# A graph network in four layers on one core: the end of each attention row in nine steps instead of six

## The chip, the cores and the metric

The kernel runs on one core of one Trainium2 chip. The metric is the device time of one execution in microseconds (us), median of several runs. Five engines matter: TensorE (PE, with its weight loads shown apart as PEld), VectorE (DVE), ScalarE (ACT), GpSimd (POOL) and SyncE (SP), whose queue starts most of the transfers. Each engine takes its instructions in the order in which they were built; an instruction that waits holds up everything behind it on its engine.

## What is computed

Four graph layers work on x (4096 x 64) with one matrix adj (4096 x 4096). After each comes a residual sum and a layer norm. adj has some 1.6% entries that are not zero, all of them positive here. The part that matters is layer 1, in the reference:

```python
hw = h @ W
h_plus = (node_adj > 0).astype(hw.dtype) @ hw          # and h_minus for < 0
e_plus = leaky_relu(concat([h_plus, h_minus], 1) @ a)  # and e_minus
att = softmax(where(edge_adj > 0, e_plus, where(edge_adj < 0, e_minus, -9e15)), axis=1)
edge_support = att * edge_adj @ hw
edge_output = gru_cell(node_support, h, ...)           # from (A > 0) @ h and (A < 0) @ h
node_output = gru_cell(edge_support, h, ...)
x = layernorm(x + d_edge * edge_output + d_node * node_output)
```

Layer 0 is a Chebyshev filter (three products with adj), layer 2 a decaying sum over each row's last hundred neighbours, layer 3 a hyperbolic aggregation.

## The kernel before, in words

adj is handled in 8 groups of 512 rows by 8 chunks of 512 columns. Layer 0 turns every tile and puts it into device memory as adj_t; the later stages load tiles of 1 MB from there.

**Attention** (the function attention, L1022) goes through 64 tiles, groups 7 to 0, chunks 0 to 7 within each. I call the eight chunks of one group a row. For each tile:
- SP loads it (L1039 or load1, L482).
- DVE makes pos, a 0/1 copy of the positive entries (L489), two chunks ahead of its use, in a ring of three buffers.
- PE multiplies pos with the split features (wide, p_ps, L1080) and the tile itself with the features (weighed, a_ps, L1089), four and eight matmuls.
- ACT, or DVE on the diagonal, makes an fp8 mask of the nonzero entries (L1045, L1047), which goes out to mask_t for the decay stage.

When a row's eight chunks are summed, p_ps and a_ps are copied out (L1140, L1143), and what is left for these 512 nodes is small and sequential: the **row's end**, built by group_end (L825). Its parts run on alternating engines:
- edge_gates (PE, L853 and L860), edge_tanh (ACT, L869), edge_rest (DVE, L874 to L876);
- scores (DVE), tanh_n (ACT, L897) and score_exps (ACT, L924 and L925), shares (DVE), new_state for the edge (DVE, L900 to L902);
- gathered (PE, L950), shared, which writes gin (ACT, L959), node_gates (PE, L853), node_sum (DVE, L883), node_tanh (ACT, L887), node_rest (DVE, L892 and L894), tanh_n, new_state for the node;
- summed (DVE, L971 and L974) and the layer norm: statistics on DVE, a square root on ACT (L275, with a table load), the rest on DVE (L277 to L288);
- decay_parts, the split of the result into three bf16 parts (DVE, L243 to L247, L994), and decay_copies (POOL's queue, L1001).

The row's end isn't issued at once. It is a list of **steps**; one step is popped behind each chunk of the next row ("if steps: steps.pop(0)(ps_p)"), so that the small work lies among the matmuls. Before the change the list has six: the edge half, the gathering, the node half with the norm, nothing, decay_parts, decay_copies. The list of a row is appended behind its eighth chunk; steps that are left when the 64 tiles are done are issued then, one after the other. The first row carries four other steps. A scheduler then orders the instructions of each engine; most matmuls and the pos, mask and diagonal instructions keep the written order.

The positive and the signed case are two branches (If and Else) in the program; only the first runs here. At its end each engine jumps over the other branch to the **decay stage** (layer 2). There PE counts masks (cnt_ps, L1355), ACT (L1360) or DVE (L1362) turns a count into weights wt, and PE gathers with them. cnt_ps is one buffer for each half, so the next count waits until the wt before has read it. The end of the last group, group 0, is issued in that stage by the same group_end with by_ln=True, as 25 small steps (L1329).

Of the kernel before, what the change touches and what calls it, by code (L numbers as in the profile page):

```python
# [14 lines left out]
AF = mybir.ActivationFunctionType  # L15
# [47 lines left out]
def gnn4_kernel(  # L63
# [21 lines left out]
    nc = tc.nc  # L85
# [120 lines left out]
    def gblocks(g):  # L206
        return slice(g * GB, (g + 1) * GB)
# [48 lines left out]
    def over_rows(t, n=F):  # L256

        return t.unsqueeze(2).to_broadcast([P, GB, n])

    def layernorm(dst, y, by_ln=False, by_scale=False):  # L260

        st = sm.tile([P, GB, 6], F32, name="ln_st")
        mv = sm.tile([P, GB, 2], F32, name="ln_mv")
        for b in range(GB):
            nc.vector.bn_stats(st[:, b, :], y[:, b, :])
            nc.vector.bn_aggr(mv[:, b, :], st[:, b, :])
        ve = sm.tile([P, GB], F32, name="ln_ve")
        s = sm.tile([P, GB], F32, name="ln_s")
        r = sm.tile([P, GB], F32, name="ln_r")
        nc.vector.tensor_scalar_add(ve, mv[:, :, 1], LN_EPS)  # L270
        if by_ln:
            nc.scalar.activation(s, ve, AF.Ln)
            nc.scalar.activation(s, s, AF.Exp, scale=0.5)
        else:
            nc.scalar.activation(s, ve, AF.Sqrt)  # L275

        nc.vector.reciprocal(r, s)  # L277
        nc.vector.tensor_tensor(r, ve, r, ALU.mult)
        nc.vector.tensor_tensor(s, s, r, ALU.add)
        nc.vector.reciprocal(r, s)  # L280
        nc.vector.tensor_scalar_mul(r, r, 2.0)
        if by_scale:
            nc.vector.scalar_tensor_tensor(s, mv[:, :, 0], -1.0, r, ALU.mult, ALU.mult)
            for b in range(GB):
                nc.scalar.activation(dst[:, b, :], y[:, b, :], AF.Identity, bias=s[:, b : b + 1], scale=r[:, b : b + 1])
            return
        nc.vector.tensor_tensor(dst, y, over_rows(mv[:, :, 0]), ALU.subtract)
        nc.vector.tensor_tensor(dst, dst, over_rows(r), ALU.mult)  # L288

    def layernorm_steps(dst, y):  # L290

        mv = sm.tile([P, GB, 2], F32, name="ln_mv")
        ve = sm.tile([P, GB], F32, name="ln_ve")
        s = sm.tile([P, GB], F32, name="ln_s")

        def spread_of():
            st = sm.tile([P, GB, 6], F32, name="ln_st")
            for b in range(GB):
                nc.vector.bn_stats(st[:, b, :], y[:, b, :])
                nc.vector.bn_aggr(mv[:, b, :], st[:, b, :])  # L300
            nc.vector.tensor_scalar_add(ve, mv[:, :, 1], LN_EPS)

        def root():
            nc.scalar.activation(s, ve, AF.Ln)
            nc.scalar.activation(s, s, AF.Exp, scale=0.5)

        def normed():
            r = sm.tile([P, GB], F32, name="ln_r")
            nc.vector.reciprocal(r, s)
            nc.vector.tensor_tensor(r, ve, r, ALU.mult)  # L310
            nc.vector.tensor_tensor(s, s, r, ALU.add)
            nc.vector.reciprocal(r, s)
            nc.vector.tensor_scalar_mul(r, r, 2.0)
            nc.vector.tensor_tensor(dst, y, over_rows(mv[:, :, 0]), ALU.subtract)
            nc.vector.tensor_tensor(dst, dst, over_rows(r), ALU.mult)

        return spread_of, root, normed
# [40 lines left out]
    wih_pp = const.tile([P, H3 + 4], F32, name="wih_pp")  # L358
    wih_mm = const.tile([P, H3 + 4], F32, name="wih_mm")
# [157 lines left out]
    with tc.tile_pool(name="acc", bufs=1) as acc_p, tc.tile_pool(  # L517
# [10 lines left out]
        part = before.rearrange("p b f -> p (b f)")[:, 0 : N // 2].rearrange("p (b f) -> p b f", b=NB)  # L528
# [258 lines left out]
    nat_b = tr_a[:, N // 2 : N].rearrange("p (b f) -> p b f", b=NB)  # L787
    middle = ctx.enter_context(ExitStack())
    late = middle.enter_context(tc.tile_pool(name="late", bufs=1))
# [19 lines left out]
    last_p = [late.tile([P, GW], F32, name=f"last_p{q}") for q in range(2)]  # L809
    last_a = late.tile([P, GW], F32, name="last_a")  # L810
    wq = late.tile([P, 2, H3], F32, name="wq")
# [13 lines left out]
    def group_end(g, Q, nb, tl, sums, a_t, wq, by_ln=False):  # L825
# [8 lines left out]
        edge = tl.tile([P, GB, F], F32, name="edge")  # L834
        node = tl.tile([P, GB, F], F32, name="node")
        cnt = e[:, :, 2 : 2 + Q]
        xg = nat_a[:, gblocks(g), 0:F]
        got = {}
# [60 lines left out]
        def new_state(dst):  # L899
            nc.vector.tensor_tensor(dst, xg, n, ALU.subtract)  # L900
            nc.vector.scalar_tensor_tensor(dst, rz[:, :, F : 2 * F], 1.0, dst, ALU.add, ALU.mult)
            nc.vector.scalar_tensor_tensor(dst, dst, 0.5, n, ALU.mult, ALU.add)  # L902
# [75 lines left out]
        def normed(part):  # L978
            def step(ps_p):
                if part == 0:  # L980
                    got["norm"] = layernorm_steps(nat_b[:, gblocks(g), :], got["y"])
                got["norm"][part]()

            return step

        if by_ln:
            norm = [[summed, normed(0)], [normed(1)], [normed(2)]]
        else:
            norm = [[summed, lambda ps_p: layernorm(nat_b[:, gblocks(g), :], got["y"])]]

        def decay_parts(ps_p):

# [12 lines left out]
        def of(h, *parts):  # L1005
            return lambda ps_p: [part(ps_p, h) for part in parts]

        return [
            [of(0, edge_gates)], [of(0, edge_tanh)], [of(0, edge_rest), of(1, edge_gates)], [of(1, edge_tanh)],
            [of(1, edge_rest), scores], [tanh_n, score_exps], [shares], [lambda ps_p: new_state(edge)],  # L1010
        ], [
            [of(0, gathered)], [of(0, shared), of(1, gathered)], [of(1, shared)],
        ], [
            [of(0, node_gates)], [of(0, node_sum)], [of(0, node_tanh)], [of(0, node_rest), of(1, node_gates)], [of(1, node_sum)], [of(1, node_tanh)],
            [of(1, node_rest)], [tanh_n] + ([to_ln] if by_ln else []), [lambda ps_p: new_state(node)],
        ] + norm, [[nothing]], [[decay_parts]], [[decay_copies]]

    def steps_of(parts):

        return [lambda ps_p, part=part: [work(ps_p) for step in part for work in step] for part in parts]  # L1020

    def attention(signed, cols_p, sg, tl, ps_a, ps_p):  # L1022
# [86 lines left out]
        for n, (g, c) in enumerate(order):  # L1109
# [27 lines left out]
            if c == NCH - 1:  # L1137
                w_t = [tl.tile([P, GW], F32, name=f"p_t{q}") for q in range(Q)] if g else last_p
                a_t = tl.tile([P, GW], F32, name="a_t") if g else last_a
                nc.scalar.copy(w_t[0], wide_ps[0])  # L1140
                if signed:
                    nc.vector.tensor_copy(w_t[1], wide_ps[1])
                nc.scalar.copy(a_t, a_ps)  # L1143
                if g:
                    steps += steps_of(group_end(g, Q, 2, tl, list(zip(w_t, (wih_pp, wih_mm))), a_t, wq))
# [152 lines left out]
    with tc.tile_pool(name="mask2", bufs=3) as mk_p, tc.tile_pool(name="wt2", bufs=3) as wt_p, tc.tile_pool(  # L1298
# [18 lines left out]
        def gather_lo(jb, half, wt, acc):  # L1317
# [8 lines left out]
                ))  # L1326


        seam = steps_of(  # L1329
            [step]  # L1330
            for part in group_end(0, 2, 1, late, list(zip(last_p, (wih_pp, wih_mm))), last_a, wq, by_ln=True)
            for step in part
        )
        gathers = []
        busy = False
        for turn, groups in enumerate(turns_of):
# [71 lines left out]
    with tc.tile_pool(name="o3", bufs=1) as op, tc.tile_pool(name="cols3", bufs=3) as cols_p, tc.tile_pool(  # L1408
# [95 lines left out]
        def turn(n):  # L1504

            t, h = n
            i, j = tiles[t]
            work = []
            if i == j:
                tp = ps_p.tile([P, GW], F32, name="post", tag="post")  # L1510
                for k in range(HB):
                    for b in range(HB):
                        nc.tensor.transpose(tp[:, cols(HB * k + b)], fs[t][:, b, cols(HB + k)], ident)
                to = own[t][:, HB:CB, 0 : HB * P]
                work.append(lambda: nc.vector.tensor_tensor(to, tp.rearrange("p (k i) -> p k i", k=HB), to, ALU.mult))  # L1515
                return work
            for b in (HB * h, HB * h + 1):
                tp = ps_p.tile([P, GW], F32, name="post", tag="post")
                for k in range(CB):
                    nc.tensor.transpose(tp[:, cols(k)], fs[t][:, k, cols(b)], ident)  # L1520
                to = mirrored[t][:, b, :]
                work.append(lambda to=to, tp=tp: nc.vector.tensor_tensor(to, tp, to, ALU.mult))  # L1522
            return work
# [137 lines left out]
        while n < NU + 2 or turns or gathers:  # L1661
# [39 lines left out]
            late = turn(late_turns.pop(n)) if n in late_turns else []  # L1701
# [65 lines left out]
```

## Time and profile before

| | us |
|---|---|
| median of 3 runs | 1482.99 (1481.95 to 1486.22) |
| the profiled execution | 1476.74 |
| its span | 1474.4 |
| attention, from the first row's edge gates to the last adjacency matmul | 600.0 to 821.6 |
| decay stage | 822 to 1037 |
| hyperbolic layer | 1037 to 1474.4 |

The profile shows one execution. A line of the timeline or of the chain is: start, length, engine, source line, operation, what is written and read, how many; in brackets the idle time ahead of it and what ended it. A line of the waits is: who waited for whom, us in total, how often, the longest. The clock column is the share of full clock that TensorE was granted.

### The profile page before, as it was taken

The page shows a single profiled execution, that of the slowest core. Times are in us where ns is not written, and L with a number is a line of the kernel's source. Part 1 is how long each engine was busy: PE and PEld are TensorE (multiplying, and loading weights), DVE is VectorE, ACT ScalarE, POOL GpSimd, SP SyncE. Part 2 cuts the span into 40 slices and gives each one's busy share as a digit, 9 for nine tenths or more (in the row PEclk, how much of TensorE's full clock was granted, in tenths as well). Part 3 has the DMA queues.
Part 4 walks back from the last instruction along what each step waited for, and adds up shares of the span by engine and source line. Part 5 has one row for each costly group of instructions (what it writes and reads, how often), then busy time and mean ns, then how long its engine had stood idle before and what let it go on. Part 6 is the DMA issues. An engine that isn't in the chain of part 4 may idle for free.

```text
span 1474.4 us, 19118 instructions
## 1 busy us (share of the span) xinstructions
PE 1340.4 (91%) x6868; PEld 617.4 (42%) x6868; DVE 1050.0 (71%) x2008; ACT 804.0 (55%) x1331; POOL 108.4 (7%) x169
## 2 busy tenths in 40 slices
PE   5899999999999988899999899999788899988984
PEld 3455555555344323444444333333333334333443
DVE  5989998887343256666777312445999999999995
ACT  3554444433000114644432377554889999999993
POOL 4111111100133000011110000000000000000000
PEclk9999999999999999999999899999899999999997
DMA  9999999999589899979887645552525444534420
GB/s 288 410 410 410 410 409 397 388 366 353 212 334 370 317 387 373 358 271 348 314 300 269 207 129 179 163 173 66 214 114 195 176 175 164 211 143 182 165 93 11
DMA packets 105662, 385.35 MB, mean 261 GB/s; under 512 B 16341, under 2 KB 17369, under 8 KB 73561
## 3 DMA queue, kind: packets, MB, share of 16 engines
q1 hardware_dynamic: 85408, 298.87, 55.2%
q0 software_dynamic: 12736, 76.29, 12.7%
q10 hardware_dynamic: 7416, 8.90, 1.7%
q8 instruction: 56, 0.92, 0.3%
q14 instruction: 46, 0.37, 0.1%
HBM read 297.26 MB, written 85.20 MB: 259 GB/s over the span
## 4 chain that ended last, share of the span: by engine, by line
PE 53%; DVE 23%; ACT 15%; DMA 6%; issue 3%; ACTq 0%; DVEq 0%; SPq 0%
PE pass L553 7%; PE w_ps L553 6%; PE tp L645 6%; PE cnt_ps L1355 4%; PE a_ps L1089 4%; PE acc_ps L1311 4%; PE pass L546 3%; PE p_ps L1080 3%; DMA raw<-in_adj_dram 3%; DVE at_m L1522 3%; PE h_ps L546 2%; ACT w L1673 2%; PE post L564 2%; ACT wt L1360 2%; DVE rt L1698 2%
## 5 line engine op out<-in xcount | busy, mean ns | idle before, releaser
L652 ACT COPY at<-tp 128x512 f32<-128x512 f32 x256 | 132.3, 599 | 133.7 <-issue 92.0
L1360 ACT ACTIVATE wt<-cnt_ps 128x512 uint16<-128x512 f32 x208 | 115.5, 595 | 71.5 <-PE cnt_ps L1355 66.9
L645 PE MATMUL tp<-ident,raw 128*128 128x128 f32 x1024 | 131.3, 281 | 17.3 <-POOL state_hhn L386 6.7
L1536 PE MATMUL sums_ps<-at_d,some 128*64 128x512 f32 x288 | 144.0, 620 | 2.0 <-DVE at_d L1515 1.8
L678 DVE TENSOR_REDUCE dpart<-raw 128x4 f32<-128x2048 f32 x64 | 145.4, 2272 | 0.2 <-DMA raw<-in_adj_dram 0.2
L680 DVE TENSOR_REDUCE lows<-raw 128x1 f32<-128x2048 f32 x64 | 145.4, 2271 | 0.0
L645 PEld LDWEIGHTS tp<-ident,raw 128*128 128x128 f32 x1024 | 114.7, 143 | 56.9 <-issue 30.5
L1089 PE MATMUL a_ps<-at,nat_a 128*64 128x512 f32 x512 | 125.9, 619 | 3.7 <-DVE at L1058 3.7
L1548 PE MATMUL sums_ps<-at_m,some 128*64 128x512 f32 x224 | 110.2, 615 | 0.0
L553 PE MATMUL w_ps<-at,cheb_n 128*128 128x512 f32 x224 | 101.1, 595 | 0.0
L1475 PE MATMUL v_ps<-rv,tr_a 64*128 64x512 f32 (+1 forms) x288 | 79.8, 632 | 22.6 <-DVE rt L1698 22.4
L553 PE MATMUL pass<-at,cheb_n 128*128 128x512 f32 x224 | 98.3, 596 | 0.7 <-DVE cheb_n L706 0.7
L1698 DVE SCALAR_TENSOR_TENSOR rt<-v_ps,rt 128x1024 f32<-128x1024 f32 x72 | 83.1, 1154 | 4.8 <-ACT rt L1674 4.4
L1355 PE MATMUL cnt_ps<-m,follow 128*64 128x512 fp8e4 x480 | 81.7, 391 | 4.6 <-ACT wt L1360 2.1
L1683 DVE SCALAR_TENSOR_TENSOR f<-rt,w 128x1024 f32<-128x1024 f32 x72 | 82.8, 1155 | 3.1 <-ACT rt L1709 3.0
L1686 DVE TENSOR_TENSOR at_d<-at_d,f 128x1024 f32<-128x1024 f32 x72 | 82.9, 1151 | 0.1
L1362 DVE TENSOR_SCALAR wt<-cnt_ps 128x512 uint16<-128x512 f32 x48 | 33.2, 692 | 66.1 <-PE cnt_ps L1355 66.1
L1522 DVE TENSOR_TENSOR at_m<-post,at_m 128x512 f32<-128x512 f32 x112 | 74.5, 678 | 4.4 <-PE post L1520 4.3
L1709 ACT ACTIVATE rt<-rt 128x1024 f32<-128x1024 f32 x72 | 72.4, 1005 | 9.3 <-DVE rt L1698 9.0
L1520 PE MATMUL post<-ident,f 128*128 128x128 f32 x448 | 69.6, 285 | 7.4 <-DVE at_m L1522 6.4
L1673 ACT ACTIVATE w<-w 128x1024 f32<-128x1024 f32 x72 | 72.0, 1001 | 5.5 <-DVE w L1502 5.5
L546 PE MATMUL h_ps<-at,cheb_n 128*64 128x512 f32 x288 | 74.3, 602 | 0.0
(396 smaller groups left out, 2276.9 us busy)
## 6 DMA issues: line engine op xcount, KB each, us to landing
at<-adj_t SPq DMA_DIRECT2D x122, 1024.0 KB, 7.0
raw<-in_adj_dram SPq DMA_DIRECT2D x64, 1024.0 KB, 13.7
adj_t<-at POOLq DMA_DIRECT2D x64, 1024.0 KB, 8.0
at_d<-adj_t SPq DMA_DIRECT2D x36, 1024.0 KB, 4.6
at_m<-adj_t SPq DMA_DIRECT2D x28, 1024.0 KB, 6.7
m<-mask_t SPq DMA_DIRECT2D x120, 128.0 KB, 2.8
m<-mask_t SPq DMA_DIRECT2D x60, 256.0 KB, 3.8
mask_t<-mask ACTq DMA_DIRECT2D x28, 256.0 KB, 6.8
```

The lines of the kernel that those rows point to most:

```text
L546: in_order(nc.tensor.matmul(ps[q * F : (q + 1) * F, :], lhsT=cheb_n[:, jb, k, :], rhs=rhs, start=first, stop=last, skip_group_check=True,))
L553: in_order(nc.tensor.matmul(ps, lhsT=cheb_n[:, jb, k : k + 2, :], rhs=rhs, start=first, stop=last))
L645: in_order(nc.tensor.transpose(tp[:, cols(b)], raw[:, b, cols(k)], ident))
L652: nc.scalar.copy(at[:, k, :], tp)
L678: in_order(nc.vector.tensor_reduce(dpart[:, g, c, :], raw, AX.X, ALU.add))
L680: in_order(nc.vector.tensor_reduce(lows[:, n : n + 1], raw.rearrange("p b j -> p (b j)"), AX.X, ALU.min))
L1089: in_order(nc.tensor.matmul(ps[q * F : (q + 1) * F, :], lhsT=nat_a[:, c * CB + k, 0:F], rhs=of[q if signed else 0][:, k, :], start=(c == 0 ...
L1355: in_order(nc.tensor.matmul(cnt[a][r * HP : (r + 1) * HP, :], lhsT=follow, rhs=chunks[c][odd][2 * a + r][:, k, :], start=(h == 2 * NB - 1) ...
L1360: in_order(nc.scalar.activation(wt[odd][a], cnt[a], AF.Relu, scale=-128.0))
L1522: work.append(lambda to=to, tp=tp: nc.vector.tensor_tensor(to, tp, to, ALU.mult))
L1536: in_order(nc.tensor.matmul(bank[0:F, :], lhsT=nat_c[:, j * CB + k, :], rhs=own[t][:, k, :], start=(i == j and k == 0), stop=(j == seq[-1] ...
L1698: nc.vector.scalar_tensor_tensor(rt, vs[n][:, :, cs], (1.0 + V_FLOOR) * SCALE, rt, ALU.max, ALU.add)
```

## The change

- The row's end in attention is divided into nine steps instead of six. A step ends where another engine takes over; the two halves (h = 0, 1) of each part go together. One step is popped behind each chunk, as before.
- The layer norm of these rows is no longer one function but the three parts of layernorm_steps (statistics, root, rest); the root keeps Sqrt where by_ln is not set.
- The end of the last group (by_ln=True) has the same steps in the same order as before; only its list is written out in another way.

```diff
-    def layernorm_steps(dst, y):
+    def layernorm_steps(dst, y, by_ln):
...
         def root():
+            if not by_ln:
+                nc.scalar.activation(s, ve, AF.Sqrt)
+                return
             nc.scalar.activation(s, ve, AF.Ln)
             nc.scalar.activation(s, s, AF.Exp, scale=0.5)
...
-        if by_ln:
-            norm = [[summed, normed(0)], [normed(1)], [normed(2)]]
-        else:
-            norm = [[summed, lambda ps_p: layernorm(nat_b[:, gblocks(g), :], got["y"])]]
+        norm = [[summed, normed(0)], [normed(1)], [normed(2)]]
...
         return [
-            [of(0, edge_gates)], [of(0, edge_tanh)], [of(0, edge_rest), of(1, edge_gates)], [of(1, edge_tanh)],
-            [of(1, edge_rest), scores], [tanh_n, score_exps], [shares], [lambda ps_p: new_state(edge)],
-        ], [
-            [of(0, gathered)], [of(0, shared), of(1, gathered)], [of(1, shared)],
-        ], [
-            [of(0, node_gates)], [of(0, node_sum)], [of(0, node_tanh)], [of(0, node_rest), of(1, node_gates)], [of(1, node_sum)], [of(1, node_tanh)],
-            [of(1, node_rest)], [tanh_n] + ([to_ln] if by_ln else []), [lambda ps_p: new_state(node)],
-        ] + norm, [[nothing]], [[decay_parts]], [[decay_copies]]
+            [[of(0, edge_gates, edge_tanh), of(1, edge_gates, edge_tanh)]],
+            [[of(0, edge_rest), of(1, edge_rest), scores, tanh_n, score_exps]],
+            [[shares, lambda ps_p: new_state(edge), of(0, gathered), of(1, gathered)]],
+            [[of(0, shared, node_gates), of(1, shared, node_gates)]],
+            [[of(0, node_sum, node_tanh), of(1, node_sum, node_tanh)]],
+            [[of(0, node_rest), of(1, node_rest), tanh_n]],
+            [[lambda ps_p: new_state(node)], *norm[:2]],
+            [norm[2], [decay_parts]],
+            [[decay_copies]],
+        ]
```

More of the change, by code (lines that the diff above doesn't have):

```diff
@@ L980, in step @@
                 if part == 0:
-                    got["norm"] = layernorm_steps(nat_b[:, gblocks(g), :], got["y"])
+                    got["norm"] = layernorm_steps(nat_b[:, gblocks(g), :], got["y"], by_ln)
                 got["norm"][part]()
             return step
-        if by_ln:
-            norm = [[summed, normed(0)], [normed(1)], [normed(2)]]
-        else:
-            norm = [[summed, lambda ps_p: layernorm(nat_b[:, gblocks(g), :], got["y"])]]
+        norm = [[summed, normed(0)], [normed(1)], [normed(2)]]
         def decay_parts(ps_p):
@@ L1006, in of @@
             return lambda ps_p: [part(ps_p, h) for part in parts]
-        return [
-            [of(0, edge_gates)], [of(0, edge_tanh)], [of(0, edge_rest), of(1, edge_gates)], [of(1, edge_tanh)],
-            [of(1, edge_rest), scores], [tanh_n, score_exps], [shares], [lambda ps_p: new_state(edge)],
-        ], [
-            [of(0, gathered)], [of(0, shared), of(1, gathered)], [of(1, shared)],
-        ], [
-            [of(0, node_gates)], [of(0, node_sum)], [of(0, node_tanh)], [of(0, node_rest), of(1, node_gates)], [of(1, node_sum)], [of(1, node_tanh)],
-            [of(1, node_rest)], [tanh_n] + ([to_ln] if by_ln else []), [lambda ps_p: new_state(node)],
-        ] + norm, [[nothing]], [[decay_parts]], [[decay_copies]]
+        if by_ln:
+            return [[step] for step in [
+                [of(0, edge_gates)], [of(0, edge_tanh)], [of(0, edge_rest), of(1, edge_gates)], [of(1, edge_tanh)],
+                [of(1, edge_rest), scores], [tanh_n, score_exps], [shares], [lambda ps_p: new_state(edge)],
+                [of(0, gathered)], [of(0, shared), of(1, gathered)], [of(1, shared)],
+                [of(0, node_gates)], [of(0, node_sum)], [of(0, node_tanh)], [of(0, node_rest), of(1, node_gates)],
+                [of(1, node_sum)], [of(1, node_tanh)], [of(1, node_rest)], [tanh_n, to_ln],
+                [lambda ps_p: new_state(node)],
+            ] + norm + [[nothing], [decay_parts], [decay_copies]]]
+        return [
+            [[of(0, edge_gates, edge_tanh), of(1, edge_gates, edge_tanh)]],
[8 more added lines that the diff above has]
+        ]
     def steps_of(parts):
@@ L1326, in gather_lo @@
                 ))
[L1329 to L1333, printed above, removed]
+        seam = steps_of(group_end(0, 2, 1, late, list(zip(last_p, (wih_pp, wih_mm))), last_a, wq, by_ln=True))
         gathers = []
```

## The prediction

> **What bounds the kernel now.** I read the busy table first, then busy time in stretches, then the waits, the chain of waits, and last the timeline at the seam where attention hands over to the decay stage.
>
> ```profile
> PE 1340.4 (91%) x6868; PEld 617.4 (42%) x6868; DVE 1050.0 (71%) x2008; ACT 804.0 (55%) x1331; POOL 108.4 (7%) x169
> ```
>
> TensorE sets the pace, so a gain must come from its idle time or its clock. The changed path runs only in attention. Cutting that stage at each row's edge gates (L853) gives one stretch per row of eight chunks:
>
> ```profile
> 600.00:636.20 36.20, 31.79 (x134) 14.08 (x130) 23.77 (x71) 21.12 (x25) 5.64 (x4) 0.91 0.87 331
> 636.20:670.60 34.40, 30.75 (x132) 14.35 (x131) 23.41 (x71) 16.95 (x22) 3.38 (x4) 0.95 0.77 285
> 733.00:763.40 30.40, 28.86 (x130) 13.38 (x130) 23.68 (x71) 11.12 (x19) 3.73 (x4) 1.00 0.87 317
> 600.00:821.60 221.60, 203.86 (x888) 93.90 (x884) 161.76 (x494) 91.42 (x139) 25.99 (x28) 0.98 0.81 296
> ```
>
> Columns are length, then PE, PEld, DVE, ACT and POOL busy, the granted clock, DMA share, GB/s. PE idles 221.60 - 203.86 = **17.7 us**; the first two rows also ran below full clock. DVE is busy only 23.7 of 30.4 us in a row: it is not full, it is late. The waits name it, and the chain shows how:
>
> ```profile
> PE p_ps L1080 <- DVE pos L489: 12.0, 7, 3.1
> PE a_ps L1089 <- DVE at L1058: 3.7, 1, 3.7
> ```
> ```profile
> 743.82 0.39 DVE gin L883
> ...
> 746.03 0.43 ACT n L897
> ...
> 748.32 0.87 DVE y L974 x4
> ...
> 751.91 1.23 DVE first_pos L489
> 753.14 0.04 issue
> 753.18 2.33 PE p_ps L1080 x8
> 755.51 1.87 PE a_ps L1089 x8
> ```
>
> From 743.82 to 751.91, 8.1 us, DVE does one row's whole node half and norm, waiting twice for ACT; the next pos stands behind it. PE has two chunks of pos in hand, worth 2 x (1.12 + 1.87) = 6.0 us, and stands 1.5 us. By the gaps in PE's timeline the seven rows lose 4.4, 3.7, 3.2, 1.6, 1.5, 1.9 and 1.5 us, again 17.7.
>
> The seam today:
>
> ```profile
> 818.18 0.28 DVE L247 CAST sup_lo<-sp_rest 128x256 bf16<-128x256 f32 x1
> 819.62 1.94 PE L1089 MATMUL a_ps<-at,nat_a 128*64 128x512 f32 x8
> 821.60 0.59 ACT L1143 COPY last_a<-a_ps 128x512 f32<-128x512 f32 x1 [1.29 <-PE a_ps L1089]
> 822.96 0.69 DVE L1362 TENSOR_SCALAR wt<-cnt_ps 128x512 uint16<-128x512 f32 x1 [4.50 <-PE cnt_ps L1355]
> 824.57 0.60 ACT L1360 ACTIVATE wt<-cnt_ps 128x512 uint16<-128x512 f32 x1 [2.38 <-DMA m<-mask_t]
> 825.22 1.07 PE L1355 MATMUL cnt_ps<-at,follow 128*64 128x512 fp8e4 x4 [2.36 <-ACT wt L1360]
> ```
>
> DVE has finished its row work (sup_lo, 818.46) before the last adjacency matmul ends (821.56; call it T). The second count matmul waits until both wt have read the first: that is T + 3.7.
>
> **What the change removes: the clumps.** A row gets nine steps and a chunk pops one. On DVE the longest run without a pos becomes new state, sum and spread (746.48 to 750.27 in the row above, 3.8 us), or norm and split (1.7 + 1.9 = 3.6). Both are below 6.0. I walked the changed instruction order through the middle rows by hand with durations of that row. Each chunk is 1.12 + 1.87, edge gates 3.0, gathered 1.16, node gates 1.06. Each pos came out 2.9 us or more ahead of its matmul. So the idle goes, 17.7.
>
> The low clock goes with it: four p_ps took 2.07 in place of 1.12 and eight a_ps 3.22 in place of 1.87 right behind the 2.41 us gap at 625; eight a_ps took 3.81 behind the 3.65 us gap at 657. That is 0.95 + 1.35 + 1.94 = 4.2. Together **21.9 us** at most.
>
> I don't count all. In the row at 670 ACT's sqrt waited behind a mask pass whose load took 5.08 us in the chain, with DMA at 0.92; finer steps don't cure a late load, and denser PE work asks for loads sooner. I keep that row's 3.15 and one 0.55 wait for gin as not gained: 3.7. Gain 18.2 (bounds: 0, if ACT makes each pos as late as now, and 21.9).
>
> What is only regrouped costs nothing. Instructions are the same in number: 14 table loads before and after, 1.28 us each, all on ACT, which is busy 11 of 30 us. SP has the same loads, a few mask loads exchanged with a neighbour. POOL issues the same copies. Cover gone, one ACT table load late in a row would cost up to 1.3.
>
> **What it adds: a tail.** Nine steps against eight pops put each row one chunk further behind. Seven rows bring 63 steps; rows 6 to 0 pop 56. Seven steps of group 1 are left for the end, behind T. The built order confirms it: after the last a_ps PE has gathered and node gates, ACT gin, both tanh and the sqrt, DVE everything from node_sum to the bf16 split. All of it stands ahead of the engines' jump to the decay stage, and behind it in each queue wait the first wt. By rows of before:
> - edge gates end 3.0 us before T. From there to the last share, the row at 733 took 735.98 to 741.81, less two pos (2.3) that no longer stand among them, plus last_p's copy (0.59) ahead of the tanh: 4.1, so T + 1.1.
> - issue 0.1, then gin to the end of spread, 741.93 to 750.27: 8.3.
> - sqrt and norm to 751.99: 1.7. Split and bias, 754.18 to 757.29 less a pos (1.17): 1.9.
> - DVE is free at T + 13.1.
> - DVE's jump. No row shows it exposed. ACT's does: 2.38 us idle between last_a and its first wt, with the count matmul done at 822.86. Bounds 0 (DVE's sequencer could run ahead) and 2.4; I take 2.4, the same jump on the nearest engine.
> - wt 0.69: PE goes on at T + 16.2, in place of T + 4.2 (825.22 plus half of the cold 1.07).
>
> That is 12.0 later. But PE's gathered and node gates (1.16 + 1.06) no longer stand before T, so T itself is 2.2 earlier. **Tail 9.8** (7.4 if the jump is hidden). Behind it nothing else is late: mask loads for chunk 6 are issued from T + 0.9 and first used at 844.8, 19 us after the second count; POOL's copies of group 1 land in 2.5 us and serve blocks 4 to 7, near the end of the turn. PE is cold at the seam in both (0.52 granted from 825.2 to 835.0), so I add nothing for it.
>
> [...]
>
> **Sum.** -21.9 + 3.7 + 9.8 = **-8.4 us**. The profiled execution took 1476.74 (span 1474.4 plus 2.3 around it), which gives 1468.3. It lay 6.25 below the median 1482.99, to which the same difference gives **1474.6**. A measurement here tells a change from none from about 0.3% on, 4.4 us.
>
> **Rivals.**
> - *The tail eats the gain.* Each of the seven rows keeps 1.5 us, as the last rows show now, because a step's DVE part still waits for ACT with a pos behind it: 10.5 stay, gain 11.4, less 9.8: 1481.4. For it: seven ACT or PE waits a row remain on DVE, each ACT mask pass is 1.9. Against: the 2.9 us in hand.
> - *Slower.* The wait moves rather than goes: before each piece DVE waits for ACT, and ACT's queue has mask passes (1.9) and their DMA issues ahead of gin, tanh and sqrt. If two passes (3.8) stand there, the 2.9 in hand is used up in each row. It decides from the point where rows keep over 12.1 of the 21.9, since the tail's 9.8 is paid whatever they do. With 19 kept: +6.9, 1489.9. For it: the row at 670, where it happened. Against: in the changed order the passes that stand there are of chunks whose pos has already been made, so their data is in.
> - *All of it.* No stall left and DVE's jump hidden: -21.9 + 7.4 = -14.5, 1468.5. It is the forecast's lower end.
>
> **Chances.** Forecast with its lower end 0.62, tail eats it 0.25, slower 0.13. The forecast's own range is 1468 to 1478.5. For 8 in 10 the range takes in the first rival whole and the lower part of the slower one: 1468 to 1488; some 0.1 lies above it, 0.08 below. Faster by over 0.3% 0.62, within 0.25, slower 0.13.
>
> **What would show it.** Right: between the first edge gates and the last a_ps PE idles under 5 us, the wait of p_ps for pos nearly vanishes, the clock there is 1.00, and nine chunks with one row's steps take about 32 us. At the seam DVE's split ends some 13 us behind the last a_ps, and PE is idle for about 10 us ahead of the second count matmul. Wrong: gaps of 1.5 us in every row (first rival), DVE waits for ACT ahead of late pos (second), or a second count that doesn't wait for DVE, which would mean that the tail is covered and my 9.8 too large.

## The result and the profile after

Four runs took 1460.58 to 1465.81 us, median **1464.19**, beside a median of 1482.47 for the kernel before on the same chip: ratio 0.988 (95% interval 0.986 to 0.990), 18.3 us faster. The profiled execution took 1463.77 (span 1461.8), 13.0 less than that of before. The direction was as forecast (-8.4); the time is below the range.

Two places are to be compared: the rows of attention and the seam behind them. Line numbers of the changed kernel are higher by 3 from L306 on and by some 12 from attention on (pos L489 is L492, p_ps L1080 is L1092, the count L1355 is L1363).

Busy time in stretches of the kernel after, cut at the edge gates as before: length, then PE, PEld, DVE, ACT, POOL busy, the granted clock, DMA share, GB/s. A stretch is now nine chunks with one row's end; the last line is the whole stage up to the last adjacency matmul.

```profile
635.70:666.90 31.20, 31.20 (x141) 14.73 (x140) 27.43 (x78) 19.22 (x24) 3.84 (x5) 1.00 1.00 372
729.80:761.10 31.30, 31.30 (x144) 14.82 (x142) 25.85 (x73) 8.76 (x17) 4.19 (x5) 1.00 0.95 335
603.90:798.20 194.30, 194.30 (x871) 91.41 (x870) 152.79 (x453) 85.94 (x129) 19.98 (x24) 1.00 0.90 333
```

PE's busy time equals the length: no idle is left, and the granted clock is 1.00 in every row (nine chunks take 31.1 to 31.8 us). From the first edge gates to T the stage went from 221.2 to 194.3 us, 26.9 less. The waits of the same window show DVE ahead of PE where it had been late:

```profile
DVE pos L492 <- PE p_ps L1092: 7.6, 4, 3.5
```

The timeline of the kernel after at the seam (T is now 798.16):

```profile
796.22 1.94 PE L1101 MATMUL a_ps<-at,nat_a 128*64 128x512 f32 x8
...
804.42 1.16 PE L1363 MATMUL cnt_ps<-at,follow 128*64 128x512 fp8e4 x4 [2.85 <-issue]
...
811.15 0.29 DVE L247 CAST sup_lo<-sp_rest 128x256 bf16<-128x256 f32 x1
811.74 0.60 ACT L1368 ACTIVATE wt<-cnt_ps 128x512 uint16<-128x512 f32 x1 [3.89 <-DMA m<-mask_t]
...
812.39 0.64 PE L1363 MATMUL cnt_ps<-at,follow 128*64 128x512 fp8e4 x2 [6.81 <-ACT wt L1368]
...
814.94 0.69 DVE L1370 TENSOR_SCALAR wt<-cnt_ps 128x512 uint16<-128x512 f32 x1 [3.50 <-issue]
815.68 0.64 PE L1363 MATMUL cnt_ps<-at,follow 128*64 128x512 fp8e4 x2 [2.65 <-DVE wt L1370]
```

DVE's split ends at T + 13.3 instead of before T. DVE's first wt stands 3.5 us behind it, and the second half of the second count, which overwrites what this wt reads, begins at T + 17.5 in place of T + 4.2. PE stands 6.81 and 2.65 us around the first half of that count, 9.5 together. So the tail is there: 13.3 us.

### The profile page after: what moved, and what is told of

Same layout as the page of the kernel before. It is cut to its first block, busy times and chain, and to the rows that moved or that the text cites. A ratio compares the mean times of both kernels' runs of the same rounds, so it can differ in the third digit from the quotient of the medians.

```text
span 1461.8 us, 19131 instructions
## 1 busy us (share of the span) xinstructions
PE 1333.6 (91%) x6868; PEld 618.0 (42%) x6868; DVE 1051.4 (72%) x2008; ACT 803.0 (55%) x1331; POOL 104.4 (7%) x169
## 4 chain that ended last, share of the span: by engine, by line
PE 55%; DVE 20%; ACT 15%; DMA 6%; issue 3%; ACTq 0%; DVEq 0%; SPq 0%
PE a_ps L1101 8%; PE pass L556 7%; PE w_ps L556 6%; PE tp L648 5%; PE p_ps L1092 4%; PE cnt_ps L1363 4%; PE acc_ps L1323 4%; DMA raw<-in_adj_dram 4%; PE pass L549 4%; DVE lows L683 3%; DVE dpart L681 3%; DVE at_m L1530 2%; ACT w L1681 2%; DVE f L1691 2%; ACT w L1492 2%
## 5 line engine op out<-in xcount | busy, mean ns | idle before, releaser
L1544 PE MATMUL sums_ps<-at_d,some 128*64 128x512 f32 x288 | 140.5, 607 | 2.4 <-DVE at_d L1523 1.8
L1101 PE MATMUL a_ps<-at,nat_a 128*64 128x512 f32 x512 | 120.8, 604 | 0.0
L1363 PE MATMUL cnt_ps<-m,follow 128*64 128x512 fp8e4 x480 | 81.8, 391 | 4.9 <-ACT wt L1368 2.3
## 6 DMA issues: line engine op xcount, KB each, us to landing
raw<-in_adj_dram SPq DMA_DIRECT2D x64, 1024.0 KB, 13.3
```

The source lines that it names most:

```text
L1101: in_order(nc.tensor.matmul(ps[q * F : (q + 1) * F, :], lhsT=nat_a[:, c * CB + k, 0:F], rhs=of[q if signed else 0][:, k, :], start=(c == 0 ...
L1363: in_order(nc.tensor.matmul(cnt[a][r * HP : (r + 1) * HP, :], lhsT=follow, rhs=chunks[c][odd][2 * a + r][:, k, :], start=(h == 2 * NB - 1) ...
L1544: in_order(nc.tensor.matmul(bank[0:F, :], lhsT=nat_c[:, j * CB + k, :], rhs=own[t][:, k, :], start=(i == j and k == 0), stop=(j == seq[-1] ...
```

## The experiments

My theory: the gain comes from dividing DVE's long runs, and the left-over steps give a part of it back at the seam. Rivals: that one part of the division alone does it; that the tail is covered; that how far ahead a step stands matters rather than how it is cut. The kernel before ran beside each set of kernels; its medians were 1480.62 (the first four below: eight steps, the tail, the node half, the norm's rest), 1479.74 (eight steps with less pos, the two with the branch reduced, the second profile) and 1479.55 us (the others).

### No tail: eight steps

```diff
-            [norm[2], [decay_parts]],
-            [[decay_copies]],
+            [norm[2], [decay_parts, decay_copies]],
```

> The changed kernel with its last two steps joined (split of the result and POOL's copies of it in one step): eight steps for eight chunks, so at the end of attention nothing is left over. Main theory (breaking DVE's 8 us run brought the gain, the seven left-over steps gave some 11 us of it back): the changed kernel's median 1464.2 less 11, so 1453, 2.0% under the kernel before; in the trace no idle of PE between the first edge gates and T, and the second count about T + 4. Rival (the tail is covered, or it costs only the engines' jump, which stays): 1461 to 1464. Rival (eight steps lengthen a step again, and clumps return): PE idle of 1 us or more per row, 1460 or more.

1455.24 us (1453.52 to 1459.16), ratio 0.984 (0.981 to 0.986). The theory said 1453, half a us below the lowest run; both rivals lie at 1460 or above, over the highest. In its stretches (one row, now of eight chunks, and the whole stage) PE has no idle:

```profile
719.80:748.75 28.95, 28.95 (x130) 13.36 (x128) 23.62 (x73) 12.43 (x20) 2.11 (x3) 1.00 0.92 327
603.90:803.79 199.89, 199.88 (x886) 92.44 (x885) 162.21 (x494) 90.36 (x138) 19.49 (x26) 1.00 0.89 324
```

221.2 less 199.9 is **21.3**, the gain of the division by itself, and the second count stands at T + 4.0 (3.7 before). The changed kernel's stage is shorter still (194.3), but only 2.6 of these 5.6 us are work moved behind T; see below.

### The tail without the gain

```diff
-        ], [
-            [of(0, gathered)], [of(0, shared), of(1, gathered)], [of(1, shared)],
-        ], [
+        ], [[nothing]], [
+            [of(0, gathered)], [of(0, shared), of(1, gathered)], [of(1, shared)],
+        ], [[nothing]], [
...
-        ] + norm, [[nothing]], [[decay_parts]], [[decay_copies]]
+        ] + norm, [[nothing]], [[nothing]], [[decay_parts]], [[decay_copies]]
```

> The kernel before with three empty steps put among its six (edge, nothing, gather, nothing, node with norm, nothing, nothing, split, copies): nine steps with the clumps of before, so that seven steps (from the gathering on) are left for the end of attention. This is the tail without the gain. Main theory: PE's idle in the rows stays near 18 us, and the tail's 11 come on top: 1493.5, 0.7% slower. Rival (the tail is covered or the comparison of the two profiles over-states it): within 3 us of before, 1482.5. Rival (the gain comes from later, not finer steps: more room between an edge half and a node half): faster, about 1470.

1495.14 us (1494.66 to 1496.25), ratio 1.011 (1.009 to 1.014): slower by 14.5, where the theory had 11, and neither covered nor faster. The second count comes at T + 17.4, nearly as in the changed kernel. Empty steps bought nothing: PE idles 21.5 us in the rows, 3.8 more than before, so the 14.5 are not the tail alone.

### Only the node half divided

```diff
             [
                 [of(0, edge_gates)], [of(0, edge_tanh)], [of(0, edge_rest), of(1, edge_gates)], [of(1, edge_tanh)],
                 [of(1, edge_rest), scores], [tanh_n, score_exps], [shares], [lambda ps_p: new_state(edge)],
             ],
             [[of(0, gathered)], [of(0, shared), of(1, gathered)], [of(1, shared)]],
             [
                 [of(0, node_gates)], [of(0, node_sum)], [of(0, node_tanh)], [of(0, node_rest), of(1, node_gates)],
-                [of(1, node_sum)], [of(1, node_tanh)], [of(1, node_rest)], [tanh_n], [lambda ps_p: new_state(node)], *norm,
-            ], [[nothing]], [[decay_parts]], [[decay_copies]],
+                [of(1, node_sum)], [of(1, node_tanh)], [of(1, node_rest)], [tanh_n],
+            ],
+            [[lambda ps_p: new_state(node)], *norm[:2]],
+            [norm[2], [decay_parts]],
+            [[decay_copies]],
```

> The kernel before with only its node half divided: edge as one step, gather as one, node gates to tanh, then new state with sum and statistics and root, then the norm's rest with the split, then the copies. Six steps, nothing left over, DVE's longest run cut between ACT's tanh and the new state. Main theory (the 8 us run was the whole stall): nearly all of the gain without the tail, 1482.5 less 24, so 1458. Rival (the edge and gather parts, 4 to 6 us of DVE with waits for ACT in between, make stalls of their own once the node half is cut): half of it, about 1470, with idle of PE ahead of chunk 1 of each row.

1469.02 us (1467.52 to 1473.41), ratio 0.993 (0.991 to 0.995): half of the gain, the rival's 1470. In the waits of its attention PE still stops for pos, and DVE for the tanh of the undivided edge half. (A line: who waited for whom, us in total, times, longest.)

```profile
PE p_ps L1095 <- DVE pos L492: 7.4, 6, 1.6
PE p_ps L1095 <- DVE first_pos L492: 4.9, 3, 2.7
```
```profile
DVE e L877 <- ACT rz L872: 33.4, 12, 5.6
```

From new state on the pieces are those of the changed kernel, while the piece from the node gates to the tanh still holds what is there in three steps; 12.3 us of waits remain. In the later rows PE's gap (1.0 to 1.1 us) stands behind norm and split, a piece that the changed kernel has too and covers. By my reading DVE comes to it there with a lead over PE, and here without one, having waited for the tanh of the edge half with pos behind it. By its profile the stage takes 214.7 us, 6.5 less than in the first profile of the kernel before; 4.0 us more of its gain lie behind T, where the clock stayed at 1.00 (last section).

### Only the norm's rest moved to the next step

```diff
-        ] + norm, [[nothing]], [[decay_parts]], [[decay_copies]]
+        ] + norm[:2], [norm[2]], [[decay_parts]], [[decay_copies]]
```

> The kernel before with only the norm's last part (after the root) moved to the next step, in the place of the empty one: six steps, nothing left over, DVE's longest run 8.1 less 1.7 less its wait for the root. Main theory: the run left is some 6.0 us, as long as the two chunks of pos in hand (6.0), so most of the 1.5 to 2 us in the later rows goes and part of the first rows' 3 to 4: gain 8 to 12, about 1472. Rival (the root in steps is the whole of it, since the wait for ACT's square root is what makes pos late): 1458. Rival (it does nothing, the edge parts do it): 1482.

1477.78 us (1473.89 to 1482.31), ratio 0.998 (0.997 to 1.000): at most a small gain, the third rival's answer. In its trace the later rows still lose 1.5 us each. The root in steps alone is not what the change lives on; my expected 8 to 12 us were wrong.

### Only the edge and gather parts divided

```diff
             [[shares, lambda ps_p: new_state(edge), of(0, gathered), of(1, gathered)]],
-            [[of(0, shared, node_gates), of(1, shared, node_gates)]],
-            [[of(0, node_sum, node_tanh), of(1, node_sum, node_tanh)]],
-            [[of(0, node_rest), of(1, node_rest), tanh_n]],
-            [[lambda ps_p: new_state(node)], *norm[:2]],
-            [norm[2], [decay_parts]],
+            [
+                [of(0, shared, node_gates)], [of(1, shared, node_gates)],
+                [of(0, node_sum, node_tanh)], [of(1, node_sum, node_tanh)],
+                [of(0, node_rest), of(1, node_rest), tanh_n], [lambda ps_p: new_state(node)], *norm,
+            ],
+            [[nothing]],
+            [[decay_parts]],
             [[decay_copies]],
```

> The complement of the kernel with the node half divided: the edge and gather parts in three steps as in the changed kernel, the whole node half with the norm in the fourth, then nothing, split, copies: seven steps, nothing left over. Theory 1 (DVE's 8 us run of the node half makes the stall): the last rows keep their 1.5 us, only the first rows' larger ones go, gain 8 to 11: about 1470. Theory 2 (it is DVE's waits for ACT's tanh in the undivided edge half, 33 us in the rows before, with pos behind them, which the node half's division left as they were): nearly the whole gain, 1455 to 1460. With 12 of 18 us of idle left where only the node half was divided, theory 2 is the likelier for at least half.

1500.72 us (1499.43 to 1501.72), ratio 1.014 (1.010 to 1.017): **slower** than before by 21, which neither theory had. Its timeline, one row, DVE's instructions:

```profile
752.99 1.22 DVE L492 TENSOR_SCALAR first_pos<-at 128x2048 fp32r<-128x2048 f32 x1
759.38 1.02 DVE L886 TENSOR_TENSOR gin<-gin,post 128x384 f32<-128x384 f32 x2 [4.89 <-PE post L856]
...
767.46 2.35 DVE L492 TENSOR_SCALAR pos<-at 128x2048 fp32r<-128x2048 f32 x2
```

The step holds one more exchange than before, since the gather's gin (shared) went in with the node half. DVE now waits 4.89 us for PE's node gates and then does the 8.1 us run, 13.3 us without a pos, and PE stands 3.2 us in the later rows, 5 to 7 in the first three. By my reading a step is as long as the exchanges between engines in it, and not only as the work in it.

### One chunk of pos less in hand

```diff
-        lead = 0 if signed else 2
+        lead = 0 if signed else 1
```

In the eight-step kernel:

> The eight-step kernel with pos made one chunk ahead in place of two, so that PE has 3.0 us in hand and not 6.0. If the clumps are covered by what PE has in hand, the two runs of DVE without a pos (3.8 and 3.6 us) now stick out by 0.6 to 0.8 each, more where they stand next to each other: 1 to 2.5 us in each of seven rows, and the clock falls behind the longer gaps: 1455.2 plus 10 to 20, so 1465 to 1475. Rival (how far ahead pos is made doesn't matter, only the order of the pieces does): 1455 to 1458, no idle in the rows.

And in the kernel before:

> The kernel before with pos made one chunk ahead in place of two. By the reasoning on record (PE stands as long as DVE's run lasts beyond the pos in hand, 8.1 against 6.0) taking away one chunk costs 3 us more in each of seven rows, 21, and more low clock: 1480 plus 21 to 28, so 1501 to 1508. Rival (how far ahead pos is written doesn't set the cover; where the pieces of the row's end stand between the pos does): within 5 of 1480.

Eight steps: 1455.71 us (1452.54 to 1459.76), no change, and no idle in the rows, the rival's answer. In the kernel before: 1524.80 (1522.81 to 1527.68), ratio 1.029 (1.025 to 1.033), 45 us slower, twice what I expected: the later rows lose 6.0 us or more in place of 1.5, so the missing chunk costs about 4.5 a row and the clock falls with it (0.89 granted over the stage). So the cover of two chunks was real in the kernel before, and the eight-step kernel doesn't need it. The loss is more than a chunk's 3.0 us; in its waits DVE's own for the tanh of the edge half grew too, from 34.7 to 61.9 us.

### The jump over the signed branch

These two kernels leave out the signed case.

```diff
     for signed in (False, True):
         with cmp.Else() if signed else tc.If(all_positive > 0) as block:
             cmp = block
+            if signed:
+                nc.vector.memset(last_a, 0.0)
+                continue
```

In the changed kernel:

> The changed kernel with the signed branch, which doesn't run here, reduced to one small memset (so it leaves out the signed case): at the end of attention each engine jumps over next to nothing. Main theory (the tail ends in an exposed jump of DVE: 3.5 us between the bf16 split and the first wt, and ACT's 3.9): DVE's idle between split and wt goes under 0.5 us, the second count comes about 3 us earlier than T + 17.5, median 1464.2 less 3, so 1461. Rival (the 3.5 us is something else, such as a wait of wt for its count): the gap stays and the time too.

And in the kernel before:

> The kernel before with the signed branch reduced to one small memset (it leaves out the signed case). There DVE's first wt ends 1.3 us after ACT's jump began, so only ACT's 2.38 us stands in the open. Main theory: ACT's idle ahead of its first wt goes under 0.5, the second count comes at T + 2 in place of T + 3.7, median 1481 less 2, so 1479. Rival (the jump costs nothing and ACT waits for the mask's transfer, which the profile names): no change.

After: 1459.60 us (1457.76 to 1464.99), ratio 0.987 (0.984 to 0.990). The timeline behind the split, with T at 795.14:

```profile
805.25 0.60 ACT L1371 ACTIVATE wt<-cnt_ps 128x512 uint16<-128x512 f32 x1 [0.42 <-DMA m<-mask_t]
...
808.12 0.29 DVE L247 CAST sup_lo<-sp_rest 128x256 bf16<-128x256 f32 x1
808.83 0.69 DVE L1373 TENSOR_SCALAR wt<-cnt_ps 128x512 uint16<-128x512 f32 x1 [0.41 <-DMA m<-mask_t]
```

DVE's 3.50 became 0.41, ACT's 3.89 became 0.42, PE's own 2.85 vanished, and the second count came 3.1 us earlier (T + 14.4). The interval of the time overlaps that of the changed kernel, so the 3 us are shown in the trace and not in the medians.

Before: 1474.58 us (1470.57 to 1476.90), ratio 0.997 (0.994 to 0.999), 5 us in place of the expected 2. ACT's 2.38 became 0.55 and the second count came 1.8 us earlier, as expected. From there to the first count on a mask loaded in this stage it takes 15.5 us in place of 19.6; these 4.2 us go with the clock. Eight microseconds behind the second count, first in the kernel before, then with the branch reduced:

```profile
826.00:834.00 8.00, 8.00 (x26) 3.93 (x24) 1.49 (x6) 3.31 (x6) 0.00 (x0) 0.50 0.83 261
```
```profile
827.00:835.00 8.00, 7.93 (x56) 3.37 (x53) 1.71 (x7) 5.58 (x10) 0.00 (x0) 1.00 0.82 265
```

In the same 8 us PE gets 26 records done at 0.50 and 56 at 1.00.

### A second profile of the kernel before

> The kernel before once more, unchanged, to see how its profiled execution varies. The first one lay at 1476.7, 6 us under the median of its runs. If the stalls of the first rows and the cold matmuls behind them differ from run to run, another execution shows other gaps at 620, 655 and 689 and a time between 1475 and 1486; if the rows agree within 1 us, the spread lies in other stages.

1482.63 us, 5.9 above the first profiled execution. From the first edge gates to T it took 225.6 in place of 221.2. The rows agree to some 0.4 us except the one at 670, which is 4.0 longer: PE's gap there is 5.73 in place of 3.14. Its timeline:

```profile
690.43 1.91 ACT L1047 ACTIVATE mask<-at 128x2048 fp8e4<-128x2048 f32 x1 [4.03 <-DMA at<-adj_t]
...
694.26 0.18 DVE L277 RECIPROCAL ln_r<-ln_s 128x4 f32<-128x4 f32 x1 [3.71 <-ACT ln_s L275]
...
696.90 2.08 PE L1080 MATMUL p_ps<-pos,parts 128*128 128x512 f32 x4 [5.73 <-DVE pos L489]
```

A load that comes late holds ACT's mask pass (4.03, against 1.44 in the first profile), behind it the table load and the root, whose input was ready at 690.23 (the root runs from 694.02 on), behind these DVE's norm, then pos, then PE, which comes back slower (four p_ps in 2.08 in place of 1.19; in the first profile the four of 2.07 at 625 stand at a granted clock of 0.50). Three other kernels of this study have these rows nearly or wholly as before: in their profiles the gap is 6.2 (the seam filled, below), 3.4 (only the norm's rest moved) and 3.0 (the branch reduced). So the stall is there in each of these executions and varies in size. What makes the load late stays open.

### The seam, filled

```diff
                 if odd:
+                    if turn == 0 and h == 2 * NB - 1:
+                        seam.pop(0)(ps_p)
                     continue
```

In the eight-step kernel:

> The eight-step kernel with the first step of the last group's end (its edge gates, some 3 us of matmuls that need only last_p) put between the first and the second pair of counts in the decay stage. PE now stands 2.3 to 2.65 us there while ACT jumps over the signed branch, and runs at half clock for 10 us behind it. Theory (the pause at the seam is what makes PE cold there; where the branch was made empty the pause went from 2.36 to 0.52 and the count after it stayed at full clock): the gates fill the pause, no cold stretch, second edge gates about T + 11 to 13 in place of T + 17.4, gain 4 to 6: 1455.5 less 5, so 1450. Rival (PE goes cold anyway, or the ACT queue, where a table load now stands between the two wt, delays the third count by as much): 1454 to 1457.

And in the kernel before:

> The same move in the kernel before, with its six steps: the seam alone. Theory: the same 4 to 6 us, so 1480 less 5, 1475; the rows keep their 18 to 22 us of idle. Rival (the pause at the seam is worth nothing): 1480.

Eight steps with it: **1449.59 us** (1448.13 to 1453.12), ratio 0.979 (0.976 to 0.983), the fastest version here, 30 us under the kernel before. The 8 us behind its second count are at full clock:

```profile
806.00:814.00 8.00, 8.00 (x60) 3.27 (x57) 3.51 (x31) 4.37 (x11) 0.00 (x0) 1.00 0.82 257
```

The second edge gates come at T + 8.6 in place of T + 17.4. Of these 8.8 us 6.2 are left at the end of the decay stage: from T to the matmul with which the hyperbolic layer sets in (behind a wait of 3.38 us for DVE's rt, in both) it is 212.7 us in place of 218.9. In the kernel before the move gives 1478.02 (1472.87 to 1480.32), ratio 0.998 (0.996 to 1.000): a small gain at best. Yet in its profile the same stretch is shorter by 5.9 us too (212.6 in place of 218.4). That profile has the larger stall at 670 (6.2 us) and from that matmul to the end 437.5 us in place of 434.4, which the edit doesn't touch; why ten runs show so little of the 5.9 stays open.

## Why the prediction was too small

The terms, by the profiled executions. The first measured value is the eight-step kernel's stage against that of before; the next two are what the changed kernel's stage has beyond it (194.3 against 199.9).

| term | on record | measured |
|---|---|---|
| idle and low clock removed | -18.2 | -21.3 |
| gathered and node gates moved behind T | -2.2 | -2.6 |
| pieces standing at cheaper places | 0 | -3.0 |
| second count, from T | +12.0 | +13.3 |
| to the second count | -8.4 | -13.6 |
| start of the stage (later by 3.5), and all behind the second count | 0 | +3.5 - 2.5 |
| span | -8.4 | -12.6 |
| median | -8.4 | -18.3 |

The line "start of the stage" is chance rather than the change: in the profiles of this study the first edge gates stand anywhere from 599.5 to 606.2 us, and of the -2.5 the hyperbolic layer makes -3.0, which no edit touches and which is 431.4 to 437.5 us long in them. The two nearly cancel.

- **What bounds it: right.** DVE late with pos, PE idle, the clock behind the longer gaps (0.91 and 0.95 in the first two rows). What was to show it came: no idle, no wait of p_ps for pos, clock 1.00, 31.1 to 31.8 us for nine chunks.
- **The step that failed first: the 3.7 kept as not gained.** I took the row at 670 to be a late load that finer steps can't cure. The load is late, but it only hurt because the root was wanted so early. That row in the kernel before, then with eight steps:

```profile
685.89 1.91 ACT L1047 ACTIVATE mask<-at 128x2048 fp8e4<-128x2048 f32 x1 [1.44 <-DMA at<-adj_t]
...
688.11 0.17 DVE L270 TENSOR_SCALAR ln_ve<-ln_mv 128x4 f32<-128x4 f32 x1
...
688.18 1.28 ACT L275 ACT_TABLE_LOAD   x1 [0.39 <-ACT mask L1047]
...
689.72 0.18 DVE L277 RECIPROCAL ln_r<-ln_s 128x4 f32<-128x4 f32 x1 [1.12 <-ACT ln_s L275]
```
```profile
682.36 1.28 ACT L305 ACT_TABLE_LOAD   x1 [0.39 <-ACT mask L1058]
...
684.93 0.17 DVE L301 TENSOR_SCALAR ln_ve<-ln_mv 128x4 f32<-128x4 f32 x1
...
685.13 0.21 ACT L305 ACTIVATE ln_s<-ln_ve 128x4 f32<-128x4 f32 x1 [1.49 <-DVE ln_ve L301]
```

  In the kernel before statistics (ln_ve) end 17.8 us behind the row's edge gates (670.5 to 688.3), the mask pass has left ACT only 0.5 us before, the root's table load has just begun, and DVE waits 1.12 us for the root with pos behind it. With eight steps they end 23.2 us behind (661.9 to 685.1), when ACT has done its pass and its table load and waits for DVE. With nine steps a pass stands ahead of the root again (687.9 to 689.8, in the row at 667), but the norm's rest is in the next step, and DVE makes a mask, a diagonal and a pos before it comes to it; no wait of DVE for the root shows there. So the upper bound of 21.9 was nearly the value: 21.3 came, and 0.6 in place of 3.7 was kept.
- **The second error is the larger one, and the same stall has a part in it: 5.3 of the 9.9 us between -8.4 and -18.3.** I added the difference of two profiled times to a median 6.25 us higher, as if these 6 us were left alone. They were partly this stall, 3.1 us in the profile I had and 5.7 or 6.2 in two others; a change that removes it gains more against the median than against a lucky execution. Of the 18.3 of the medians, 13.0 are in the two profiles; a profile of before with the larger stall (1482.63) stands 18.9 above that of after. How often the larger stall comes isn't known.
- **3.0 us I had not thought of.** In the kernel before each piece of PE work stands at the same place in every row; with nine steps it moves by one chunk a row. Consecutive chunks swap their two matmul groups, so a piece can split two a_ps groups or stand between two p_ps groups. By the trace after, edge gates take 3.00 at the one place and 2.77 at the other, the gathering 1.50 and 1.16 to 1.27 (1.9 us in all), and seven fewer pairs of a_ps are split (3.58 for sixteen together, 2 x 1.87 apart: 1.1). On record this term stood at nothing: pieces that are only regrouped were said to cost the same. No run tested it by itself.
- **The tail: right, one term too small.** DVE free at T + 13.3 (13.1 on record). DVE's jump: I took 2.4 from ACT's; it is 3.5. The reduced branch shows that it is the jump. POOL's copies landed in 6.0 us by the median of the profile after, and not in 2.5; no wait of PE for them shows.
- **The reason that 6.0 us of cover suffice: too simple.** I compared DVE's longest run with the pos in hand. In the kernel before that cover is real (one chunk less costs 45 us), but with the node half alone divided the same short runs leave 12 us of waits, and with all divided 3.0 us of cover do as well as 6.0. What would fit all six divisions is that time is lost with the exchanges between engines that one pop holds, since the next pos waits through all of them; the slowest division here (+21) has the most in one pop. That is a reading; no run changed the number of exchanges alone.
- **The rivals.** "The tail eats the gain" and "slower" would have needed the rows to keep 10.5 and 19 us; they kept none. "All of it" (1468.5) was the nearest; it had no stall left, which came true, and DVE's jump hidden, which didn't.

## What to carry to other kernels

When small sequential work is slipped in between large pieces, try steps that hold one exchange between engines each, and no more of them than there are pieces behind which they are issued: one more, and the last group's work falls behind the end. Here that put the second count 13 us later; by the medians nine steps gain 18 us and eight gain 25. A stall that comes from a late transfer through a busy engine varies from run to run (here PE's gap is 3.0 to 6.2 us in five profiles with these rows nearly as before), so look at two profiles before a difference of profiles is added to a median. Where all engines jump at the same time, give one of them independent work there: PE's first gates between the counts took the eight-step kernel from 1455 to 1450 us, though in the kernel before the same move brought little.

## What the runs showed of the hardware

- **A jump over the other branch is not free where it stands in the open.** ACT 2.38 and 3.89 us, DVE 3.50, PE 2.85; with the branch emptied 0.55, 0.42, 0.41 and none. What the engine does in that time these traces don't show.
- **Here a short pause cost more in clock than in time.** Gaps of 0.68 and 2.36 us with 0.62 of work between them were followed by some 10 us at half clock (0.50 granted from 824.3 to 834.5), though PE was busy without a gap from 825.2 on. With the branch reduced the gaps were 0.68 and 0.52, the clock stayed at 1.00, and the way from the second count to the first one on a mask loaded in the stage took 4.2 us less. In the kernel with the node half divided, gaps of 0.94 and 2.06 at the same place left the clock at 1.00. Nor does the length of one gap decide: ahead of the third four p_ps of attention PE stands 2.24 or 2.25 us in nine of the profiles, and these four and the sixteen a_ps behind them take 1.20 and 3.65 us in five of them (the second one of before and those of the tail, the norm's rest, the edge parts and the seam filled in the kernel before) and 1.80 to 2.08 and 4.21 to 4.63 in four (the nine steps, where the granted clock of the next 10 us is 0.84, the eight steps, the node half, the branch reduced in the kernel before). What decides was not tried.
